# Layer 1's mixture of experts: where a block's outputs wait for their scatter

## The chip, the cores and the metric

The kernel runs on one core of a Trainium2 chip. The metric is the device time of one execution in microseconds, and lower is better. All data are float32. TensorE (PE) multiplies, VectorE (DVE) and ScalarE (ACT) do the elementwise work, GpSimd (POOL) mostly issues indirect DMAs here, and SyncE (SP) issues the direct ones.

## The reference

Four layers are computed in turn on 2708 rows of 256 numbers. Each layer first adds a graph product over the dense 2708 x 2708 adjacency matrix, and then a feed-forward part. The change lies in the feed-forward part of layer 1, a mixture of 8 experts with one hidden layer for all of them, in which every row goes through the expert with the greatest gate alone:

```python
def _L1_ffn_ref(x, W1, b1, Wg, bg, Wd, bd):
    H = jax.nn.gelu(xf @ W1 + b1, approximate=False)
    probs = jax.nn.softmax((H @ Wg + bg) / TEMP, axis=-1)
    assign = jnp.argmax(probs, axis=-1)
    out = jnp.zeros_like(xf)
    for e in range(Wd.shape[0]):
        y = H @ Wd[e] + bd[e]
        sel = (assign == e)[:, None]
        out = out + jnp.where(sel, probs[:, e:e + 1] * y, 0.0)
    return out.reshape(orig_shape)
```

`xf` is the layer-normalised `x`. It has 256 columns, `H` has 1024.

## The kernel before

**Layer 1.** The rows are worked in three groups (8, 8 and 6 tiles of 128 rows). For each group the graph product is summed in PSUM and added to `x`. Then `send1` normalises the rows (`normed`, which writes tiles `xn` of the pool `work`, three places in turn), turns them, computes `H` and the gate, writes the rows of `H` to a DRAM tensor `hid`, and decides where each row goes (`route`). For each row it scatters a pair, the row's number and its gate value, to the DRAM tensor `taken1` (L505), so that rows of one expert stand together.

**Blocks.** `blocks` cuts the experts' lists into blocks of 128 rows of one expert. Nine blocks (0 to 8) come from the first two groups, and their work begins while the third group is still in its gates. Fifteen more (9 to 23) come from the rest and need the third group's routing. A further set stands in a branch that is entered only if the number of blocks asks for it.

`Units.pieces` runs the blocks. For one block:

- `fetch_names` (L519, POOL) gathers the 128 pairs of row number and gate value;
- `fetch_rows` (L659, POOL) gathers the 128 rows of `hid` that they name into one of four buffers `hs`;
- `fetch` (L1054, SP) loads the expert's weights, 1152 KB with the bias in a last row, into one of three buffers `wb`. It first reads the expert's number;
- `turn` transposes the rows on PE (L670, eight transposes), and ACT copies them out of PSUM as `hTs` (L671). This is done one block ahead;
- 16 matmuls (L719) sum the 128 x 256 output in one of two PSUM banks `yacc`;
- DVE adds the bias from `wb` (L720) and multiplies by the gate value (L721). The result is `ys`, a tile of the pool of the blocks with two places in turn;
- POOL scatters its rows to the DRAM tensor `given1` (L505).

**What sets the order.** [...] A place in a pool is written again only when its last readers are done: `ys` when its scatter has landed, `hs` when the transposes of its rows are done, `wb` when L719 and L720 of its block are done. POOL issues names, rows and outputs from one queue, so an instruction that waits holds all behind it. Beside block 13 (`beside`, with n = NA + 4) PE and DVE do the few products of `centre` (L245) and DVE `score_columns` (L269, L270) for layer 2. Towards the end POOL also issues the loads of layer 2's small tensors. After the last block SP loads `given1` back (`mine`, L56), and the addition to `x` (L1413) begins layer 2. The tag `xn` is written in layer 1 by `norm_to` (L197) through `normed`; it is written again in layer 2.

Of the kernel before, what the change touches and what calls it, by code (L numbers as in the profile page):

```python
# [8 lines left out]
F32 = mybir.dt.float32  # L9
# [6 lines left out]
P = 128  # L16
N = 2708
D = 256
# [48 lines left out]
def adj_ffn4(ctx: ExitStack, tc: tile.TileContext, a: dict, out: bass.AP):  # L67
# [4 lines left out]
    work = ctx.enter_context(tc.tile_pool(name="work", reuse_waits="tile", bufs=3))  # L72
# [429 lines left out]
    def scatter(dst, ix, src, bound, group):  # L502


        i = g.indirect_dma_start(out=dst, out_offset=bass.IndirectOffsetOnAxis(ap=ix, axis=0),  # L505
                                 in_=src, in_offset=None, bounds_check=bound, oob_is_err=False)
        tc.declare_no_dep(i.ins, group=group, reason="different rows")
        tc.declare_no_dep(i.ins, group=group + "read", reason="rows that were read are not written")
        tc.add_to_no_dep_group(group, i.ins)
        scattered.setdefault(group, []).append(i.ins)  # L510
# [25 lines left out]
    class Blocks:  # L536
# [4 lines left out]
        def __init__(self, pool, given, weights):  # L541
            self.pool, self.given = pool, given
            self.weights, self.ahead, self.rows, self.at = weights, [], [], [0, 0]
            self.late, self.begun, self.made = None, None, None
            self.ik, self.ok = "taken0", "given0"
# [84 lines left out]
    class Units(Blocks):  # L630
# [3 lines left out]
        def __init__(self, pool, given, weights, hidden):  # L634
            Blocks.__init__(self, pool, given, weights)
            self.hidden, self.named, self.places, self.got = hidden, [], [0, 0], None

            self.names = pool.tile([P, MOST, 2], F32, name="names")
            g.memset(self.names, 1.0)
            self.hs = [pool.tile([P, HC * P], F32, name="hs", tag="hs", bufs=3) for _ in range(3)]  # L640
            for h in self.hs:
                g.memset(h, 0.0)
            self.ik, self.ok = "taken1", "given1"

        def fetch_names(self, item):
            (_, ix, *_), b, past, src, full = item
# [54 lines left out]
        def pieces(self, pool, during=None):  # L701

            turned = [self.turn(pool, self.rows[0][1])]
            yield
            n = 0
            while self.rows:
                if len(self.rows) > 1:
                    turned.append(self.turn(pool, self.rows[1][1]))
                    yield
                w2, hT = self.ahead.pop(0), turned.pop(0)  # L710
                m, _ = self.rows.pop(0)
                self.more()
                if during is not None:
                    during(n)
                n += 1
                y = pool.tile([P, D], F32, name="ys", bufs=2)
                q = pools["psum"].tile([P, W], F32, name="yacc", bufs=2)[:, :D]
                for f in range(HC):
                    te.matmul(q, lhsT=hT[:, f, :], rhs=w2[:, f, :], start=(f == 0), stop=(f == HC - 1))  # L719
                v.tensor_tensor(y, q, w2[:, HC, :], ALU.add)  # L720
                i = v.tensor_scalar(y, y, m[:, 1:2], None, op0=ALU.mult)  # L721
                self.last = i.ins.name
                scatter(self.given, m[:, 0:1].bitcast(I32), y, self.given.shape[0] - 1, self.ok)
                yield
# [60 lines left out]
    with ExitStack() as l0:  # L785
# [103 lines left out]
        for tiles in GROUPS:  # L889
# [8 lines left out]
            for j in range(FULL):  # L898
# [22 lines left out]
                y = gp.tile([P, GMAX * P], F32, name="y", bufs=3)[:r, :w]  # L921
# [440 lines left out]
    with tc.tile_pool(name="t3", reuse_waits="tile", bufs=1) as t3:  # L1362
# [279 lines left out]
        with tc.tile_pool(name="h2", reuse_waits="tile", bufs=2) as hp:  # L1642
# [120 lines left out]
            for c0, w in parts:  # L1763
# [11 lines left out]
                y = ypool.tile([P, 4, D], F32, name="y", bufs=2)  # L1775
# [11 lines left out]
        with tc.tile_pool(name="g3e", reuse_waits="tile", bufs=1) as ge, ExitStack() as sums:  # L1787
# [121 lines left out]
            for now, (m, j) in enumerate(slots):  # L1909
# [50 lines left out]
                for hf, (h0, q) in enumerate(halves):  # L1960
                    s.copy(oT[:, pair, hf, :q], num[:, hf, :q])
                    z, y = 2 * Q * hf, 2 * Q * pair
# [68 lines left out]
```

## The time and the profile before

| what | value |
|---|---|
| runs of the kernel before | 1935.83, 1922.75, 1929.87 us; median 1929.87 |
| profiled execution | 1912.16 us, its span 1910.4 us |
| PE, PE weight load | 1824.7 us (96%), 1323.7 us (69%) |
| DVE, ACT, POOL | 1098.8 us (58%), 642.4 us (34%), 343.8 us (18%) |
| first and last L719 | 953.6 and 1078.4 us after the span's start |
| first addition of layer 2 (L1413) | 1088.15 us |
| L720: count, median length | 24, 424 ns |
| L721: count, median length | 24, 353 ns |
| DMA from issue to landing, median: outputs, rows, names | 6.8, 7.7, 6.2 us (950 to 1086 us) |

Times of events are microseconds from the span's start. A line of the waits names the engine and the line that waited, what it waited for, the sum in us, the count and the longest. A wait for several semaphores is put down to the one that came last. In a line of the timeline the idle time before an instruction and its releaser stand in square brackets. [...]

### The profile page before, as it was taken

How to read it: one execution, taken by the hardware profiler on the slowest of the kernel's cores; microseconds unless marked ns; L12 is line 12 of the kernel's file. 1: busy time of each engine (PE TensorE's matmuls, PEld its weight loads, DVE VectorE, ACT ScalarE, POOL GpSimd, SP SyncE). 2: the span in 40 equal slices, each digit the busy share in tenths (PEclk: the TensorE clock that was granted, in tenths of full speed). 3: DMA queues.
4: the chain of work that ended last, by engine and by line, in shares of the span. 5: the costliest groups of instructions: out<-in, count | busy, mean ns of one | idle time of the engine just before them, and what ended most of it. 6: DMA issues, size and time to landing. Idle time of an engine off the chain costs nothing.

```text
span 1910.4 us, 25747 instructions
## 1 busy us (share of the span) xinstructions
PE 1824.7 (96%) x9453; PEld 1323.7 (69%) x9453; DVE 1098.8 (58%) x2498; ACT 642.4 (34%) x1459; POOL 343.8 (18%) x406
## 2 busy tenths in 40 slices
PE   7999999999998999999989799999899999999998
PEld 6888788888887888887778578887566632232344
DVE  6777873443333524454532365555354498999897
ACT  7868752222222303122312232222233551031231
POOL 1004254333321002304356200000000000000000
PEclk9999999999998999999999899999899999999999
DMA  8435657877763453644779610000101000000000
GB/s 273 142 110 156 217 191 287 333 299 294 287 255 127 151 151 101 162 116 121 215 259 360 216 40 1 1 1 1 44 1 34 17 1 23 23 15 26 20 20 16
DMA packets 90141, 243.94 MB, mean 128 GB/s; under 512 B 18159, under 2 KB 44823, under 8 KB 80792
## 3 DMA queue, kind: packets, MB, share of 16 engines
q1 hardware_dynamic: 73048, 199.80, 31.3%
q0 software_dynamic: 16960, 42.42, 6.8%
q8 instruction: 78, 1.28, 0.3%
q14 instruction: 55, 0.45, 0.1%
HBM read 216.29 MB, written 28.71 MB: 128 GB/s over the span
## 4 chain that ended last, share of the span: by engine, by line
PE 40%; DMA 4%; DVE 3%; ACT 2%; issue 1%; POOL 0%; DVEq 0%; POOLq 0%; SPq 0%; ACTq 0%
PE num L1929 10%; PE ps_acc L1502 9%; PE den L1939 6%; PE ps_tmp L367 4%; PE ps_acc L1692 3%; PE ps_tmp L260 2%; PE yacc L719 2%; DMA L_ffn_beta<-in_L_ffn_beta 1%; DMA given<-ys,names 1%; PE ps_acc L260 1%; PE ps_tmp L213 1%; DVE e L1899 1%; DMA names<-taken,b_ix 1%; DMA wb<-in_L_ffn_Wdp 0%; PE ps_acc L670 0%
## 5 line engine op out<-in xcount | busy, mean ns | idle before, releaser
L1899 DVE SCALAR_TENSOR_TENSOR e<-arena,G,mask 128x1024 f32<-128x1024 f32 (+1 forms) x264 | 286.9, 1147 | 13.7 <-PE den L1939 13.6
L1929 PE MATMUL num<-e,wh 128*64 128x512 f32 (+4 forms) x1056 | 215.8, 551 | 0.0
L929 PE MATMUL acc<-msg,wt 128*128 128x256 f32 x882 | 199.0, 382 | 2.8 <-DVE wt L887 1.5
L1502 PE MATMUL ps_acc<-hh,e 128*128 128x257 f32 x882 | 199.3, 382 | 1.9 <-ACT o L1445 1.9
L1290 PE MATMUL acc<-sup,adrow 128*128 128x256 f32 x882 | 198.4, 382 | 0.2 <-DVE adrow L1258 0.2
L929 PEld LDWEIGHTS acc<-msg,wt 128*128 128x128 f32 x882 | 165.5, 191 | 29.4 <-DVE wt L887 2.8
L1290 PEld LDWEIGHTS acc<-sup,adrow 128*128 128x128 f32 x882 | 164.8, 190 | 28.3 <-issue 5.5
L1502 PEld LDWEIGHTS ps_acc<-hh,e 128*128 128x128 f32 x882 | 163.7, 190 | 29.5 <-ACT o L1445 4.5
L583 PE MATMUL ps_acc<-xTs,wa 128*128 128x256 f32 (+1 forms) x768 | 169.4, 373 | 3.5 <-DVE xTs L573 3.4
L617 PE MATMUL yacc<-wb,hTs 128*128 128x256 f32 x736 | 168.4, 380 | 0.0
L585 ACT ACTIVATE hTs<-ps_acc,wa 128x256 f32<-128x256 f32 (+1 forms) x192 | 88.9, 465 | 236.1 <-PE yacc L617 161.9
L583 PEld LDWEIGHTS ps_acc<-xTs,wa 128*128 128x128 f32 x768 | 136.4, 190 | 29.9 <-DVE xTs L573 6.4
L1929 PEld LDWEIGHTS num<-e,wh 128*64 128x64 f32 (+1 forms) x1056 | 66.5, 136 | 127.3 <-issue 105.6
L617 PEld LDWEIGHTS yacc<-wb,hTs 128*128 128x128 f32 x736 | 137.1, 190 | 18.0 <-DVE ys L619 0.6
L1494 DVE SCALAR_TENSOR_TENSOR e<-Rb,G,mask 128x640 f32<-128x640 f32 (+2 forms) x110 | 85.0, 774 | 90.6 <-PE ps_acc L1502 90.4
L1939 PE MATMUL den<-e,wh 128*32 128x512 f32 (+4 forms) x1056 | 118.0, 548 | 0.0
L214 ACT COPY xT<-ps_tmp 128x256 f32<-128x256 f32 x98 | 33.6, 365 | 238.1 <-PE ps_tmp L213 218.9
L1255 DVE TENSOR_SCALAR mask<-adrow 128x1024 uint8<-128x1024 f32 (+1 forms) x66 | 41.1, 624 | 121.1 <-DMA adrow<-in_adjT 120.5
L719 PE MATMUL yacc<-wb,hTs 128*128 128x256 f32 x384 | 90.7, 391 | 12.3 <-DVE ys L720 7.8
L719 PEld LDWEIGHTS yacc<-wb,hTs 128*128 128x128 f32 x384 | 73.1, 195 | 24.1 <-DVE ys L720 8.8
L887 DVE SCALAR_TENSOR_TENSOR wt<-adrow,wt 128x640 f32<-128x640 f32 (+3 forms) x67 | 71.0, 1063 | 28.2 <-ACT wt L141 27.9
L1939 PEld LDWEIGHTS den<-e,wh 128*32 128x32 f32 (+1 forms) x1056 | 30.2, 108 | 77.9 <-issue 73.8
(457 smaller groups left out, 2562.6 us busy)
## 6 DMA issues: line engine op xcount, KB each, us to landing
adhalf<-in_adjT SPq DMA_DIRECT2D x42, 677.0 KB
wb<-in_L_ffn_W2p SPq DMA_DIRECT2D x24, 1152.0 KB
wb<-in_L_ffn_Wdp SPq DMA_DIRECT2D x24, 1152.0 KB
wa<-in_L_ffn_W1b SPq DMA_DIRECT2D x24, 1028.0 KB
adrow<-in_adjT SPq DMA_DIRECT2D x42, 512.0 KB
adrow<-in_adjT SPq DMA_DIRECT2D x42, 320.0 KB
adrow<-in_adjT SPq DMA_DIRECT2D x21, 576.0 KB
adrow<-in_adjT SPq DMA_DIRECT2D x21, 448.0 KB
```

The lines of the kernel that those rows point to most:

```text
L367: te.matmul(p[:, :w], lhsT=w1[:, c, f * P : (f + 1) * P], rhs=xnT[:, c, c0 : c0 + w], start=(c == 0), stop=(c == DC - 1))
L583: i = te.matmul(p[:, f % 2, : m * P], lhsT=w1[:, c, f * P : (f + 1) * P], rhs=xT[:, c, : m * P], start=(c == 0), stop=(c == DC - 1))
L585: s.activation(hT[:, f, : m * P], p[:, f % 2, : m * P], AF.Gelu, bias=bias[:, f : f + 1])
L617: te.matmul(q[:, k, :], lhsT=hT[:, f, k * P : (k + 1) * P], rhs=w2[:, f, :], start=(f == 0), stop=(f == HC - 1))
L719: te.matmul(q, lhsT=hT[:, f, :], rhs=w2[:, f, :], start=(f == 0), stop=(f == HC - 1))
L929: te.matmul(p[:q, n - pair[0], :], lhsT=wt[:, k : k + q], rhs=msg[:r, j, :], start=(j == 0 and n == pair[0]), stop=(j == FULL - 1 and n == ...
L1290: te.matmul(p[:q, n - pair[0], :], lhsT=ad[:, k : k + q], rhs=sup[:, jj, :], start=(jj == 0 and n == pair[0]), stop=(jj == FULL - 1 and n ...
L1494: i = v.scalar_tensor_tensor(e[:r, :w], Rb[:r, c0 : c0 + w], G[:r, j, :], mask[:r, j, c0 : c0 + w], op0=ALU.max, op1=ALU.mult)
L1502: te.matmul(p[:, : D + 1], lhsT=e[:, k : k + q], rhs=hh[:, j, :], start=(j == 0), stop=False)
L1899: v.scalar_tensor_tensor(e[:, :w], slow[:, m % 2, k, :w], G[:, j, 2 * pair + k, :], mask[:, j, c0 : c0 + w], op0=ALU.max, op1=ALU.mult)
L1929: te.matmul(num[k * DK : (k + 1) * DK, hf, :q], lhsT=wh[some, j, 2 * pair + k, :DK], rhs=e[some, h0 - c0 : h0 - c0 + q], start=(j == 0), s ...
L1939: te.matmul(den[z : z + Q, :q], lhsT=wh[some, i, 2 * pair + k, DK : DK + 1] .to_broadcast([some.stop - some.start, Q]), rhs=e[some, h0 - c ...
```

## The change

A counter of the blocks' outputs is kept. Of five outputs in turn, two are tiles `ys` of the pool of the blocks, as before, and three are tiles `xn` of the pool `work`, in whose three places the gates' normalised rows stood. Since `ys` has two places and `xn` three, an output's place is that of the output five blocks before it. No instruction is added or removed, and no transfer.

```diff
-            self.ik, self.ok = "taken1", "given1"
+            self.ik, self.ok, self.outputs = "taken1", "given1", 0
...
                 n += 1
-                y = pool.tile([P, D], F32, name="ys", bufs=2)
+                self.outputs += 1
+                y = (pool.tile([P, D], F32, name="ys", bufs=2) if self.outputs % 5 < 2 else
+                     work.tile([P, D], F32, name="xn"))
                 q = pools["psum"].tile([P, W], F32, name="yacc", bufs=2)[:, :D]
```

## The prediction

> **What bounds the kernel now.** I read the page for the span, the waits of the stretch from 950 to 1086 us (layer 1's blocks), then the timeline of TensorE in it, and last the windows of 5 us for the DMA engines' share. The page first:
>
> ```profile
> span 1910.4 us, 25747 instructions
> PE 1824.7 (96%) x9453; PEld 1323.7 (69%) x9453; DVE 1098.8 (58%) x2498; ACT 642.4 (34%) x1459; POOL 343.8 (18%) x406
> L719 PE MATMUL yacc<-wb,hTs 128*128 128x256 f32 x384 | 90.7, 391 | 12.3 <-DVE ys L720 7.8
> ```
>
> PE is the bound of the whole. The 384 matmuls of L719 are 24 blocks of 16, so the conditional rest did not run. A block costs PE 4.33 us in an undisturbed piece: 3.46 for L719 and 0.87 for the eight transposes of L670 (the chain of waits has both numbers). 24 of them are 103.9 us; the blocks take from 953.6 to 1078.8, 125.2 us. The waits say where part of the 21 us went (us in total, times, longest):
>
> ```profile
> DVE ys L720 <- DMA given<-ys,names: 63.3, 13, 8.8
> SPq L1054 <- DVE ys L720: 87.8, 18, 10.4
> PEld yacc L719 <- DVE ys L720: 8.8, 4, 5.3
> PE yacc L719 <- DVE ys L720: 7.8, 3, 5.0
> PE yacc L719 <- DMA wb<-in_L_ffn_Wdp: 4.5, 5, 1.7
> PE ps_acc L670 <- DMA hs<-hid,names: 2.2, 1, 2.2
> ```
>
> DVE's output of a block waits until the scatter of two blocks before has landed, for it has two places; the next weights (SPq L1054) wait for that output, because it reads the bias row of its weights; and PE, with two yacc banks, waits for it in turn. The timeline of PE (start, length, instructions, idle before and releaser) shows that only a few of the 13 waits reach PE:
>
> ```profile
> 987.45 1.04 PE L670 MATMUL ps_acc<-ident,hs 128*128 128x128 f32 x8
> 990.16 3.72 PE L719 MATMUL yacc<-wb,hTs 128*128 128x256 f32 x16 [1.67 <-DVE ys L720]
> 993.72 1.04 PE L670 MATMUL ps_acc<-ident,hs 128*128 128x128 f32 x8
> 999.80 6.58 PE L719 MATMUL yacc<-wb,hTs 128*128 128x256 f32 x16 [5.05 <-DVE ys L720]
> 1006.22 1.04 PE L670 MATMUL ps_acc<-ident,hs 128*128 128x128 f32 x8
> ...
> 1069.71 3.72 PE L719 MATMUL yacc<-wb,hTs 128*128 128x256 f32 x16 [1.04 <-DVE ys L720]
> 1075.10 3.69 PE L719 MATMUL yacc<-wb,hTs 128*128 128x256 f32 x16 [1.67 <-DMA wb<-in_L_ffn_Wdp]
> ```
>
> After the 5.05 us of idle time block 8's products take 6.58 us where others take 3.5. The windows (columns: busy time by engine, granted clock, DMA share, GB/s):
>
> ```profile
> 980.00:985.00 5.00, 4.96 (x25) 4.16 (x24) 0.78 (x2) 2.15 (x4) 2.87 (x3) 1.00 0.40 112
> 995.00:1000.00 5.00, 0.20 (x1) 0.20 (x2) 0.64 (x2) 0.48 (x1) 0.74 (x1) 0.88 0.45 170
> 1000.00:1005.00 5.00, 5.00 (x12) 4.00 (x13) 0.90 (x3) 0.00 (x0) 3.67 (x4) 0.50 0.83 298
> 1040.00:1045.00 5.00, 4.67 (x25) 4.03 (x26) 0.78 (x2) 1.35 (x4) 2.72 (x3) 1.00 0.99 405
> 1055.00:1060.00 5.00, 5.00 (x31) 4.45 (x29) 0.90 (x3) 1.53 (x3) 4.02 (x6) 1.00 1.02 420
> 1065.00:1070.00 5.00, 3.96 (x22) 3.33 (x22) 0.73 (x2) 1.64 (x4) 0.58 (x1) 1.00 0.70 289
> ```
>
> So there are three stages: up to 1005 DMA has gaps (0.40, 0.45) and PE waits for outputs; from 1005 to 1060 DMA is at 0.92 to 1.02; at the end it has gaps again.
>
> [...] clock 0.50 after 5.05 us, 1.00 after 1.67 us. [...]
>
> **The change, part by part.** Instructions of PE, ACT, SP and POOL stand in the same order before and after, with the same DMAs; on DVE, L720 and L721 only write elsewhere. No duration changes. What changes is one wait of L720: on the scatter of five blocks before instead of two.
>
> *First stage.* Block 6 ends on PE at 987.45. Then transposes 0.87, L719 of block 7 at 988.3 (before 990.16), end 991.8. The weights of block 7 were issued at 983.87, after L720 of block 4; that output's products ended at 979.8 (976.34 + 3.46, blocks counted from 0), so now at 980.3, 8.0 us ahead of use. Next late: the transposes of block 9. Their rows are gathered by POOL at 985.52, behind names that wait for the routing's scatters (landing 980.7); nothing of that moves. With the median 7.6 us of hs they land at 993.1 (4.5 to 10.5: 990.0 to 996.0). So transposes 993.1, block 8 at 994.0, end 997.4, against 1006.22: **-8.8 us**, of which 3.1 is the half clock. By the range of hs: -5.9 to -10 (PE alone would be there at 996.2).
>
> POOL hides behind that: an indirect DMA takes 1.02 + 0.31 us, three a block are 4.0, below PE's 4.33. It is behind at 984 (six routing scatters) and catches up. The new wait on five before: block 9's output (1001.9) needs the scatter of block 4, issued by POOL at 990.74, landed 999.2. It holds, with 2.7 us to spare; later ones have more.
>
> *Middle, blocks 9 to 20.* Before, 1007.10 to 1059.77 is 4.79 us a block at a DMA share of about 0.97. A block moves 1.18 MB weights, 0.52 rows, 0.13 outputs, 1.83 MB: at the 360 to 420 GB/s of full windows 4.4 to 5.1 us. So this stage is DMA's, not the output's; its waits of outputs (63.3 us, mostly here) are free. Two weight loads (blocks 9, 10) that were issued at 999.8 and 1000.6 go out at 987.9 and 992.3 now: 2.36 MB, 6.6 us of DMA at 360 GB/s. The gaps from 980 to 997.4 sum to 0.60x5 + 0.16x5 + 0.15x5 + 0.55x2.4 = 5.9 us. The 0.7 that doesn't fit, and rows that come late in the fuller queue, appear as waits for wb and hs: I take **+2 us**. Bounds: -2.8 (the four waits for wb there, 0.81 + 0.16 + 0.30 + 1.53, all gone) to +7 (both loads pushed through at full price).
>
> *End.* L720 of block 20 ran at 1069.23 though its products ended at 1063.4 (1059.77 + 3.6), behind the scatter of block 18 that POOL issued only at 1060.22, after five loads of layer 2. Now it runs at 1063.5, block 23's weights go out at 1064 instead of 1069.68 and land 5.4 us later, at 1069.4. Block 22 starts at 1068.5 (before 1069.71), block 23 at 1072, ends 1075.5 against 1078.8: **-3.3 us**; at least -1.2, at most -3.3. After that, the last scatter and the loads of layer 2 (1079.3 to 1088.2) are as before. xn is next written by ACT in layer 2's attention, long after the scatters landed: 0.
>
> Sum: -8.8 + 2 - 3.3 = **-10.1 us**, bounds -15.9 to -0.1. Against the profiled execution (1912.16, its span 1910.4) that is 1902. The median shown is 1929.87, 17.7 above that execution; nothing in the stages says the saving scales, so I subtract it: 1920.
>
> **Rivals.**
> *DMA is the bound throughout.* From 985 to 1075 its share sums to 80.2 of 90 us. If weights pushed into the first stage delay the hs of block 9 to 996 and the middle pays the full +7, the gain is 5.9 + 3.3 - 7, about 2: 1928. For it: the share of 1.0 after 1040. Against: gaps of 0.40 to 0.45 just where the loads move to. Chance 0.2.
> *PE alone is the bound.* If hs and wb are never late, the end lies at 953.6 + 103.9 + routing products 1.5, the L245 products 1.0, the wait for hs 2.6: 1062.6, a gain of 16: 1914. Against: full DMA windows need more than 4.33 us a block. Chance 0.1.
> *Slower: weights become late in every block.* A load may go out 9.0 us ahead of its use (two L719, three L670, less DVE's 0.5). In full windows it took 7.9 to 9.7 (issue 1032.13, use 1040.03; 1035.16, 1044.90). If the denser queue makes it 10.5, each of the 14 blocks from 9 to 22 waits 1.5: 21 us lost against 12.1 gained, 1939. It decides from 9.0 + 12.1/14 = 9.9 us. Against: the bytes are the same and waiting slows their issue. Chance 0.06.
> *It does nothing*, because the releaser was another (scatter and PE ends lie close): L720 started right after a landing 13 times, so hardly: 0.02, 1930.
>
> **How the numbers follow.** The forecast (gain 7 to 13) has 0.62. The likeliest time is 1920. The three times shown differ by 13 us, so I add about 4 either way to the cases: PE alone less 4 is 1910, DMA bound plus 2 is 1930: range 1909 to 1930. A difference under 1% (19 us) can't be told from none here. No case gains 19 without scatter of the runs: faster 0.08; slower 0.05; same 0.87.
>
> **What would show it.** Right: L720's waits for given near 0; no PE wait for ys; block 8 near 3.5 us at clock 1.0; waits for wb or hs up from 4.5 and 2.2; DMA share above 0.8 from 985 on; the first layer 2 addition near 1078 instead of 1088. Wrong: blocks 9 to 20 above 5.0 us each, or hs of block 9 landing after 996.

## The result and the profile after

| | before | after |
|---|---|---|
| median of 20 runs, us | 1927.05 (1918.82 to 1935.83) | 1921.84 (1916.06 to 1929.84) |
| ratio, 95% interval | | 0.997 (0.9957 to 0.9982) |
| profiled span, us | 1910.4 | 1916.0 |

The change is worth 5.8 us of 1927 by the ratio (3.5 to 8.3), a good half of the 10.1 forecast; the time lies 2 us from the 1920 predicted and well within the range. That closeness is luck in part: the forecast was taken off a median of 1929.87, 2.8 us above that of the 20 runs, and its gain was 4 to 5 us too large, so the two errors offset each other. The profiled execution of after is nevertheless 5.6 us longer than that of before. That contradiction is the first thing to clear up.

In after the lines from the products on have moved by two: L719 to L721 is L721 to L723, and L1054 is L1056. The page of after (first the span, then busy time by engine, then the row of the products):

```profile
span 1916.0 us, 25757 instructions
PE 1829.1 (95%) x9453; PEld 1327.3 (69%) x9453; DVE 1098.2 (57%) x2498; ACT 641.9 (34%) x1459; POOL 344.5 (18%) x406
L721 PE MATMUL yacc<-wb,hTs 128*128 128x256 f32 x384 | 88.9, 385 | 1.2 <-DMA wb<-in_L_ffn_Wdp 1.1
```

The idle time in front of the products fell from 12.3 us to 1.2, and none of it is an output's. The waits of after, 950 to 1086 us (total, times, longest):

```profile
DVE xn L722 <- PE yacc L721: 27.7, 8, 4.4
DVE ys L722 <- PE yacc L721: 23.5, 6, 7.0
PE ps_acc L670 <- ACT hTs L671: 7.4, 3, 3.8
PE yacc L721 <- DMA wb<-in_L_ffn_Wdp: 1.1, 1, 1.1
PE ps_acc L670 <- DMA hs<-hid,names: 0.9, 2, 0.7
```

L722 now mostly waits for its products. No line names a wait for `given`, where before had 63.3 us in 13 waits. But a line is there that before did not have: TensorE waits 7.4 us for `hTs`. The timeline of TensorE shows 5.8 us of it (columns as in the prediction):

```profile
982.31 1.04 PE L670 MATMUL ps_acc<-ident,hs 128*128 128x128 f32 x8
985.29 0.66 PE L670 MATMUL ps_acc<-ident,hs 128*128 128x128 f32 x4 [1.94 <-ACT hTs L671]
989.78 1.97 PE L670 MATMUL ps_acc<-ident,hs 128*128 128x128 f32 x8 [3.83 <-ACT hTs L671]
991.54 8.82 PE L721 MATMUL yacc<-wb,hTs 128*128 128x256 f32 x32
1000.20 0.60 PE L670 MATMUL ps_acc<-ident,hs 128*128 128x128 f32 x4
```

After 5.8 us of idle time (1.94 + 3.83) two blocks take 8.82 us, at a granted clock of 0.64 from 991.5 to 996.5, where the first profile of before has 7.07 at 1.00. I call this the stand. r5_before below, the kernel before unaltered, has it too. So it isn't the change's.

Nor is every output on time. Outputs 7, 8 and 10 begin 5.6, 2.0 and 1.6 us after the modelled end of their products:

```profile
DVE xn L722 <- PE ps_acc L670: 9.3, 2, 9.1
1014.20 0.42 DVE L722 TENSOR_TENSOR xn<-yacc,wb 128x256 f32<-128x256 f32 x1 [9.09 <-PE ps_acc L670]
```

This is output 7. A scatter hardly holds it: that of five blocks before was issued 27 us earlier. The trace has no update of TensorE's semaphore from 1004.7 to 1014.2, and then five within 0.35 us. That looks like a late signal of TensorE, and the stand does too.

**Profiles of two kinds.** All the profiles taken fall into two groups. In the first profile of before and in r9 to r12 (r9 to r12 on two chips) no such wait is seen, layer 0's blocks (first to last L583) take 334.8 to 336.2 us, and the trace holds 1455 or 1456 records of TensorE's semaphore. In after and in r1 to r8 (two chips for these eight runs) TensorE stands 4.5 to 5.9 us for `hTs` before block 4's products, layer 0's blocks take 345.7 to 349.1 us, and only 1423 to 1435 records are there. I call the groups N (no stand) and S (stand). The traces of S also lack 17 to 20% of the records of DMA landings (after has 9037, the first profile of before 11156), so what ended a wait is less sure there.

The 12 us of layer 0 look like a stand too. From 270 to 320 us TensorE is never idle in a profile of kind N. In each of the nine of kind S it is idle for 6.4 to 7.8 us and then works for 3.7 to 9.8 us at half clock; with half of these counted as lost, that is an estimate of 10 to 13 us. First a window of before, then two of r1_again:

```profile
295.00:300.00 5.00, 5.00 (x25) 4.27 (x24) 0.78 (x2) 1.90 (x4) 2.86 (x4) 1.00 0.67 197
295.00:300.00 5.00, 0.00 (x0) 0.00 (x0) 0.00 (x0) 0.00 (x0) 2.61 (x3) 0.76 0.62 242
300.00:305.00 5.00, 4.27 (x11) 3.51 (x12) 0.78 (x2) 0.00 (x0) 3.09 (x3) 0.55 0.27 76
```

The timed runs go with the chip: before took 1922 to 1927 us in the median where S was seen, 1907 to 1910 where N was. So the prediction read an execution of kind N, and its result was profiled in one of kind S; the two can't be subtracted. The table gives the stages that the prediction used, each from the trace: from the start of block 0's products to block 9's, on to block 21's, and to the end of the last.

| kernel | kind | 0 to 9 | 9 to 21 | 21 to end | sum |
|---|---|---|---|---|---|
| before, first profile | N | 53.49 | 57.08 | 14.62 | 125.18 |
| r12_before | N | 52.89 | 54.45 | 14.90 | 122.24 |
| r9_bias_before | N | 48.20 | 60.03 | 12.99 | 121.22 |
| r10_bias_after | N | 48.37 | 56.57 | 15.66 | 120.60 |
| r11_six | N | 49.80 | 59.79 | 12.38 | 121.98 |
| r5_before | S | 50.89 | 61.21 | 12.51 | 124.61 |
| r6_null | S | 51.02 | 57.69 | 14.69 | 123.41 |
| after | S | 51.19 | 55.53 | 12.71 | 119.43 |
| r1_again (after) | S | 49.61 | 58.64 | 12.89 | 121.14 |
| r2_early | S | 48.92 | 58.19 | 13.84 | 120.95 |
| r3_late | S | 50.49 | 56.42 | 12.80 | 119.70 |
| r4_three | S | 49.37 | 56.28 | 13.83 | 119.47 |

One kernel's stage differs by up to 3 us between two profiles of one kind (after and r1_again in the middle), so a stage of one profile is not read closer than that.

### The profile page after: what moved, and what is told of

Same layout as the page of the kernel before. It is cut to its first block, busy times and chain, and to the rows that moved or that the text cites. A ratio compares the mean times of both kernels' runs of the same rounds, so it can differ in the third digit from the quotient of the medians.

```text
span 1916.0 us, 25757 instructions
## 1 busy us (share of the span) xinstructions
PE 1829.1 (95%) x9453; PEld 1327.3 (69%) x9453; DVE 1098.2 (57%) x2498; ACT 641.9 (34%) x1459; POOL 344.5 (18%) x406
## 5 line engine op out<-in xcount | busy, mean ns | idle before, releaser
L1901 DVE SCALAR_TENSOR_TENSOR e<-arena,G,mask 128x1024 f32<-128x1024 f32 (+1 forms) x264 | 287.0, 1149 | 13.6 <-PE den L1941 13.6
L583 PE MATMUL ps_acc<-xTs,wa 128*128 128x256 f32 (+1 forms) x768 | 170.2, 374 | 5.4 <-DVE xTs L573 2.5
L583 PEld LDWEIGHTS ps_acc<-xTs,wa 128*128 128x128 f32 x768 | 137.1, 190 | 32.1 <-DVE xTs L573 5.4
L617 PEld LDWEIGHTS yacc<-wb,hTs 128*128 128x128 f32 x736 | 138.8, 193 | 24.4 <-issue 3.9
L721 PE MATMUL yacc<-wb,hTs 128*128 128x256 f32 x384 | 88.9, 385 | 1.2 <-DMA wb<-in_L_ffn_Wdp 1.1
L619 DVE TENSOR_TENSOR ys<-yacc,wb 128x256 f32<-128x256 f32 x46 | 19.5, 424 | 113.0 <-PE yacc L617 98.2
```

What stands on the lines that cost most here:

```text
L583: i = te.matmul(p[:, f % 2, : m * P], lhsT=w1[:, c, f * P : (f + 1) * P], rhs=xT[:, c, : m * P], start=(c == 0), stop=(c == DC - 1))
L617: te.matmul(q[:, k, :], lhsT=hT[:, f, k * P : (k + 1) * P], rhs=w2[:, f, :], start=(f == 0), stop=(f == HC - 1))
L1901: v.scalar_tensor_tensor(e[:, :w], slow[:, m % 2, k, :w], G[:, j, 2 * pair + k, :], mask[:, j, c0 : c0 + w], op0=ALU.max, op1=ALU.mult)
```

## The experiments

Blocks and outputs are numbered from 0, except that "the first nine outputs" are blocks 0 to 8. All ratios are to runs of the kernel before on the same chip.

### Which outputs bring the gain: r1 to r4

r1_again is the change unaltered. The others change only the choice of the place:

```diff
# r2_early: five places for the first nine outputs only
-  ... if self.outputs % 5 < 2 else
+  ... if self.outputs % 5 < 2 or self.outputs > 9 else
# r3_late: five places from the tenth output on
+  ... if self.outputs % 5 < 2 or self.outputs <= 9 else
# r4_three: three places, all of them xn
+  y = work.tile([P, D], F32, name="xn")
```

> The changed kernel once more, unaltered, for a second profile of the first stage: in the first one PE stood from 983 to 991.5 us between the outputs of blocks 3 and 4 and nothing in that view says for what. If that stall belongs to the change (weights pushed into a full DMA queue), it is there again, of 4 to 8 us, and the blocks take about 119 us from the first L721 to the end of the last. If it is an accident of one execution, it is gone and the blocks take 111 to 115 us. Time in either case 3 to 8 us below the kernel before.

> Five places for the first nine outputs only, two for the rest. Theory (first stage gains most): 2 to 5 us below the kernel before, block 8 without idle time for an output before it. Rival (DMA is the bound throughout, and what the first stage gains is paid back in the middle): 0 to 1 us below the kernel before. Rival (the end gains it): 0.

> Two places for the first nine outputs, five from the tenth on. Theory: only the end gains, 1 to 3.3 us below the kernel before, and the wait of 5 us with the half clock before block 8 is as in the kernel before. Rival (DMA throughout): nearly the whole gain of the change, 4 to 6 us, is here.

> Three places for all outputs, those of the normalised rows alone. Theory: a third place already takes away most of it, since a scatter lands 6.8 us (4.0 to 8.5) after its issue and a block takes 4.3 to 4.8; but where POOL is behind by up to 10 us, around block 6, part of the wait stays: 2 to 5 us below the kernel before, between it and the five places. If five places are needed all along, it is within 1 us of the kernel before.

| run | ratio | 95% interval |
|---|---|---|
| r1_again | 0.9980 | 0.9969 to 0.9992 |
| r2_early | 1.0017 | 1.0005 to 1.0029 |
| r3_late | 0.9972 | 0.9959 to 0.9984 |
| r4_three | 0.9979 | 0.9968 to 0.9989 |

On this chip, one of kind S, no gain is seen from the places of the first nine outputs, on which the prediction's largest term rested: r2 is 3.3 us slower (1.0 to 5.6), which isn't read as a loss, since r6 below leaves up to 4 us between two builds of one program. The later ones are worth all of it, 5.4 us. Both results go against the theory in their expectations, and r3 has the gain that the rival there named. A third place is already as good as five within the intervals. r3_late, which keeps two places up to block 8, has the stand too:

```profile
PE ps_acc L670 <- ACT hTs L671: 5.8, 1, 5.8
PE yacc L721 <- DMA wb<-in_L_ffn_Wdp: 3.7, 4, 1.2
```

In r3 outputs 6 and 8 still come 4.9 and 4.1 us after their products, but TensorE waits only 0.17 us for an output (before block 8; in the first profile of before output 6 came 11.7 us late, and the wait was 5.05). That POOL and the scatters catch up while TensorE stands is the likely reason; it wasn't tested.

### Is the stand the change's, and what can two builds differ by: r5 and r6

r5_before is the kernel before, unaltered. r6_null gives its two places as two tags of one place each; instructions and waits are those of before:

```diff
-  y = pool.tile([P, D], F32, name="ys", bufs=2)
+  y = pool.tile([P, D], F32, name="ys", tag=f"ys{n % 2}", bufs=1)
```

> The kernel before once more, for a second profile. All four profiles taken since show PE standing 5.8 us before the second half of block 6's transposes, which the first profile of the kernel before does not have, and so does the one whose first nine outputs use the places of before. If that stall is the kernel's own and the first profile of before was a lucky draw, it is here too, and the blocks take 124 to 132 us here from the first L719 to the end of the last. If the stall comes from the change, it is absent.

> The kernel before with its two places under two names, the same instructions and waits at other addresses, to see what a build alone is worth. If builds of the same program agree, 0 within 0.1 per cent of the kernel before. If the layout alone moves the time by 3 us either way, the differences among the runs so far can't be read to better than that.

r5_before took 1926.75 us (one run) beside 1925.82. r6_null measured 0.9995 (0.9979 to 1.0011). So a difference below some 3 us between builds can't be told from none with this number of runs, and the 5.8 us of the change are not much above it. The waits of TensorE and SP in r5_before:

```profile
PE yacc L719 <- DMA wb<-in_L_ffn_Wdp: 5.9, 5, 3.3
PE ps_acc L670 <- ACT hTs L671: 4.5, 1, 4.5
PE yacc L719 <- DVE ys L720: 0.7, 1, 0.7
SPq L1054 <- DVE ys L720: 82.6, 18, 9.2
```

The stand is there without the change. Outputs hold TensorE for 0.7 us only, against 7.8 in the first profile, but weights hold it for 5.9 (r6_null: 6.5). After has 1.1 of this, r1_again 1.2, r2_early, with two places for the later blocks, 4.3. In kind S, then, these profiles have an output's late scatter reach TensorE over SP: L720 waits for the scatter, the next load waits for L720 because a place of `wb` holds the bias too, and TensorE waits for the load.

### Is the full DMA queue the condition: r7 and r8

Half of the expert's weights, so that a load moves 640 KB instead of 1152:

```diff
-  wb = wbs["pool"].tile([P, 2048 + D], F32, name="wb", bufs=3)
+  wb = wbs["pool"].tile([P, 1024 + D], F32, name="wb", bufs=3)
-  te.matmul(q, lhsT=hT[:, f, :], rhs=w2[:, f, :], ...)
+  te.matmul(q, lhsT=hT[:, f, :], rhs=w2[:, f % 4, :], ...)
-  v.tensor_tensor(y, q, w2[:, HC, :], ALU.add)
+  v.tensor_tensor(y, q, w2[:, 4, :], ALU.add)
```

The lines are shown in part; the load is shortened to match. These two kernels leave out half of the weights, and the bias too, in whose stead a piece of the weights is added.

> The kernel before with half of each block's weights left out (four of the eight 128-row pieces are loaded and used twice), so that a block moves 1.3 MB instead of 1.83. Theory (waits for outputs cost PE beside DMA's bound): the waits of L720 for scatters stay, a scatter lands in 3 to 5 us, and the blocks take 110 to 120 us. Rival (DMA is the bound throughout): the blocks drop to PE's 104 to 110 us with two places already.

> The changed kernel with the same half of the weights left out. Theory: with DMA relieved the places are worth more than the 4 to 5 us of the whole kernels, 6 to 12 us below the halved kernel before. Rival (DMA throughout, so that the queue of transfers makes the scatters slow in the first place): less than with the whole weights, 0 to 3 us, since scatters land soon enough for two places.

r7 (two places) measured 0.9957 (0.9939 to 0.9975), r8 (five) 0.9961 (0.9945 to 0.9978): with half the bytes no gain from the places is seen, though the intervals leave room for up to 4 us. r8's theory, 6 to 12 us, is refuted; its rival's 0 to 3 fits. The blocks took 114.0 us in r7's profile, within its theory's 110 to 120, but the waits for scatters, which that theory kept, are nearly gone. A window of r7 and its wait for the scatters:

```profile
1010.00:1060.00 50.00, 48.94 (x270) 43.25 (x269) 12.07 (x33) 13.66 (x24) 34.28 (x34) 1.00 0.80 267
DVE ys L720 <- DMA given<-ys,names: 5.4, 1, 5.4
```

At a DMA share of 0.80, where r5_before has 0.94 in the same window, one output is seen to wait for a scatter, not 11 (49.4 us in r5_before). That supports the reading that two places were too few because scatters land late while the weights load. A profile of kind N agrees: in r12 the last two scatters, with no weights left to load (DMA share 0.11 and less), landed in 2.4 and 2.6 us, those of blocks 3 to 17, where the trace has them, in 5.4 to 6.9 (DMA share 0.99 from 1010 to 1060). Taking 12 MB away (24 times 512 KB) gave 8 us only by the ratio, so the bytes don't bound the whole stretch.

### Is it the weights' release: r9 to r11

r9 has two places, but the bias has a tile and a load of its own (four places), so that `wb` is freed by TensorE alone. r10 is the same edit on the changed kernel. r11 has six places, three `ys` and three `xn`. The lines are shown in part:

```diff
-  wb = wbs["pool"].tile([P, 2048 + D], F32, name="wb", bufs=3)
+  wb = wbs["pool"].tile([P, 2048], F32, name="wb", bufs=3)
+  bd = wbs["pool"].tile([P, D], F32, name="bd", bufs=4)
+  i = nc.sync.dma_start(bd, a["L1_ffn_Wdp"][bass.ds(e, 1), :, 2048:] ...)
-  v.tensor_tensor(y, q, w2[:, HC, :], ALU.add)
+  v.tensor_tensor(y, q, bd, ALU.add)
# r11_six
+  y = (pool.tile([P, D], F32, name="ys", bufs=3) if self.outputs % 6 < 3 else
```

> The kernel before, two output places, but the bias row of an expert has a tile and a load of its own (four places, 128 KB, the same bytes in all), so that a place of the weights comes free when TensorE has read it (L719) and no longer when L720 has. L720 still waits for the scatter of two blocks before. Theory A (the five places gain through the earlier release of the weights): TensorE's waits for wb fall from 4.5 to 5.9 us to below 2, and the time is 3 to 6 us below the kernel before (ratio 0.997 to 0.998). Theory B (they gain through L720 releasing the yacc banks, or through the order on DVE): no gain, within 2 us of the kernel before; waits for wb may fall, but waits of TensorE for yacc (ys) or hs take their place. Theory C (one more transfer a block on a full queue costs by itself): 2 to 6 us above.

> The changed kernel (five places) with the same separate bias tile. Theory A: nothing is left to gain, since L720 already runs right after its products: within 2 us of the changed kernel, ratio to the kernel before 0.996 to 0.999. Theory B: likewise about the changed kernel. Theory C: 2 to 6 us above the changed kernel, ratio 0.999 to 1.001. Against r9, Theory A has the two equal within 2 us, Theory B has this one 4 to 6 us lower.

> Six places in turn, three of them ys and three of them xn; nothing else is changed against five. If with five places no output waits for a scatter any more (none did in the profile of the changed kernel), this is the changed kernel again: ratio 0.996 to 0.998. If five still hold an output back in executions other than the profiled one, another 2 us or more comes off: below 0.996.

| run | places | ratio | 95% interval |
|---|---|---|---|
| r9_bias_before | 2 | 0.9983 | 0.9972 to 0.9993 |
| r10_bias_after | 5 | 0.9969 | 0.9956 to 0.9981 |
| r11_six | 6 | 0.9975 | 0.9965 to 0.9986 |

The weights' release alone gives 3.2 us of the 5.9 that r10 gives. Six places give 4.8 us, no more than five gave elsewhere (0.9970 and 0.9980), as its expectation has it. No version here is shown to beat the change. In r9 TensorE's waits for `wb` are down to 0.5 us, as Theory A has it, and the ratio lies just outside the ones it named. It still waits 4.5 us for outputs (before: 7.8, r12: 5.8) and 3.2 for rows. The middle values make the release half of the gain; the intervals leave anything from a sixth to all of it. r9's profile shows what stays when only the weights are freed. SP waits for TensorE now; then DVE's timeline, with two outputs that wait for scatters, the second ahead of layer 2's `score_columns`; and last TensorE:

```profile
SPq L1054 <- PE yacc L719: 70.0, 20, 9.8
```

```profile
1009.22 0.42 DVE L720 TENSOR_TENSOR ys<-yacc,bd 128x256 f32<-128x256 f32 x1 [4.98 <-DMA given<-ys,names]
...
1018.63 0.42 DVE L720 TENSOR_TENSOR ys<-yacc,bd 128x256 f32<-128x256 f32 x1 [3.52 <-DMA given<-ys,names]
1019.09 0.35 DVE L721 TENSOR_SCALAR ys<-ys,names 128x256 f32<-128x256 f32 x1
1019.36 0.75 DVE L269 TENSOR_TENSOR o<-w_l,L_gnn_attn_src 128x256 f32<-128x256 f32 x2
```

```profile
1021.82 2.09 PE L245 MATMUL ps_tmp<-w_l,all_ones 128*128 128x258 f32 x4 [4.18 <-DVE w_l L270]
```

L269 stands behind an L720 that waited 3.52 us for a scatter and began at 1018.63; it begins at 1019.36, and TensorE waits 4.18 us for the scores. So a late output has three ways to TensorE, the `yacc` bank, the weights, and whatever follows L720 on DVE; in r10, with five places, TensorE waits by none of them.

r10 and r11 are also the first profiles of kind N with more than two places, that is, of the execution that the prediction had worked out. TensorE in r10, from block 7 to block 9, and the windows of 5 us beside it:

```profile
989.16 3.62 PE L721 MATMUL yacc<-wb,hTs 128*128 128x256 f32 x16
997.46 1.94 PE L670 MATMUL ps_acc<-ident,hs 128*128 128x128 f32 x8 [4.68 <-DMA hs<-hid,names]
999.19 4.43 PE L721 MATMUL yacc<-wb,hTs 128*128 128x256 f32 x16
1003.46 1.04 PE L670 MATMUL ps_acc<-ident,hs 128*128 128x128 f32 x8
1004.34 3.62 PE L721 MATMUL yacc<-wb,hTs 128*128 128x256 f32 x16
```

```profile
982.40:987.40 5.00, 5.00 (x27) 4.41 (x26) 0.78 (x2) 1.07 (x2) 3.07 (x3) 1.00 1.00 355
987.40:992.40 5.00, 5.00 (x28) 4.44 (x28) 0.78 (x2) 1.07 (x2) 2.39 (x3) 1.00 0.96 358
992.40:997.40 5.00, 0.38 (x2) 0.00 (x0) 0.79 (x2) 0.00 (x0) 2.63 (x3) 1.00 0.98 324
997.40:1002.40 5.00, 4.94 (x20) 4.46 (x21) 0.00 (x0) 1.17 (x2) 2.09 (x3) 0.66 0.62 235
```

The wait for the output before block 7 or 8 is gone, as predicted. In its place TensorE waits 4.68 us for the rows of block 9, almost as long as the 5.05 us for the output before, and its clock falls as it did (0.66 in the last window; 4.43 us for a block). The windows are 26.4 us after block 0's start, like those from 980 on in before: the DMA shares, 0.40, 0.84, 0.85 and 0.45 there, have become 1.00, 0.96, 0.98 and 0.62.

### Was the 5 us wait of the first profile an accident: r12

The kernel before, unaltered, for one more profile.

> The kernel before, unaltered, for one more profile: the first profile of before and r5_before differ in the first stage, and the profiles of r9, r10 and r11 (all 1452 semaphore records of TensorE, no wait of 4 to 6 us for hTs) resemble the first one. If this execution is of the kind of r9 to r11, Theory 1 (with two places the third scatter of that stretch is late and TensorE stands 5 us for it) expects block 9 to begin 52 to 54 us after block 0 as in the first profile (53.5), against 48.4 in r10 and 49.8 in r11; Theory 2 (the 5.05 us of the first profile were that execution's own) expects 48 to 50. If it is of the kind of r5_before, it shows a wait of 4 to 6 us for hTs instead and says nothing on this.

It ran on a chip of kind N (1910.21 us, beside 1906.79) and block 9 began 52.9 us after block 0, as Theory 1 has it. TensorE in it:

```profile
999.61 6.26 PE L719 MATMUL yacc<-wb,hTs 128*128 128x256 f32 x16 [4.39 <-DVE ys L720]
```

So with two places the wait for the output before block 8 belongs to kind N (5.05 and 4.39 us). It isn't in r5_before, where the stand came first.

## Why the prediction was right, and where it was not

The time fell within the range and on the forecast's side. No rival came about as a whole. But of the three terms the first is half its size at best, and the other two measured no more than the scatter between profiles.

**The first stage, -8.8 us: the term that was mis-sized.** In kind N, block 9 starts 53.2 us after block 0 with two places (mean of two profiles) and 49.1 with five or six (r10, r11): -4.1. That isn't the places' doing alone: r9, with two places and the weights freed earlier, has 48.2, and its waits for outputs before blocks 7 and 8 are 1.67 and 1.76 us. In kind S it is 51.0 (r5, r6) against 50.4 (after, r1): -0.6.

The step that failed in kind N is "nothing of that moves", said of the names and rows of block 9. The prediction found the next late thing rightly, and the two loads did go out early: 32.5 and 36.8 us after block 0 in r10, where it had 34.3 and 38.7 and before had 46.2 and 47.1. But POOL's small transfers landed later beside them. The names of block 9 landed 2.4 us after their issue in both profiles of before of kind N, at a DMA share of 0.40 and 0.31 in these 5 us, and 4.6, 5.1 and 5.8 in r9, r10 and r11, where the share was 1.00 (r10) and 0.94 (r11); so the gather of the rows went out at 33.4 us after block 0 (r10) and 33.8 (r11) instead of 31.9, and took 8.1 and 8.7 us instead of the 7.6 assumed. It landed at 41.5 and 42.5, not 39.5. That costs 2.0 and 3.0 us.

The long wait brought back the half clock that the sum had saved (granted clock 0.66 and 0.50 in the windows after it): transposes of 1.94 us for 1.04 and products of 4.43 and 4.85 for 3.62, 1.7 and 2.1 us. Together 3.7 and 5.1: block 8 ends 47.5 and 48.9 us after block 0 (at the next transposes) where the forecast had 43.8. That is outside the term's own range, 5.9 to 10 us: its late end, rows at 996.0, left 4.2 us of idle time and yet no half clock. The sum had no term for names that land late, in 5.1 and 5.8 us against 2.4 in these profiles. What the rival of a bound DMA said of this stage, rows at 996 (42.4 us after block 0), was nearly exact; its +7 us in the middle was not paid. In kind S, where the result was timed, the names of block 9 took 6.4 to 7.5 us (six profiles) with two places and with five, and the stand replaced the wait that this term was to remove.

**The middle, +2 us.** In kind N the stretch from block 9 to 21 went from 55.8 to 58.2, +2.4, with waits for `hs` in the place of those for `wb`, as predicted: after block 9 r10 has 2.8 us of them, r11 5.1, and neither waits for `wb`. In kind S it went from 59.5 to 57.1, -2.4: there the waits for weights fell from about 6 us to about 1. Both sizes are within the 3 us by which single profiles differ. "Its waits of outputs are free" sits badly with r3, which gained 5.4 us (3.1 to 7.9) in kind S by the outputs from block 9 on alone.

**The end, -3.3 us.** -0.7 in kind N (14.8 to 14.0) and -0.8 in kind S (13.6 to 12.8). Single profiles run from 12.4 to 15.7, so no more is said than that the full 3.3 is not seen. In r10 the last block waits 2.34 us on SP's side and then takes 5.38 us for 3.62 (granted clock 0.90 from 1060 to 1080).

The sums of these means are -2.4 us (N) and -3.7 (S) of the blocks' stretch. The timed gain was 3.8 to 5.9 us (r1, after, r11, r10). In kind S the trace accounts for most of it; in kind N it is short by about half, no more than the scatter between profiles.

**Rivals.** That TensorE alone bounds the stretch is refuted by the 119 us and more that it takes in every version with all the weights, against 109. Slower by late weights: waits for weights fell. That the change does nothing: the waits for `given` are gone. That DMA is the bound throughout: right on the rows of block 9 in kind N; its +7 us in the middle isn't seen, and with half of the weights' bytes the time fell by 8 us only.

**Readings and sums.** The 13 waits for scatters (63.3 us) stood on DVE; TensorE waited for outputs three times (7.8 us). By its own terms the lower bound of the sum is -16.1, not -15.9.

**The gap that should have been read.** The sum was made against an execution 17.7 us below the median of the runs, and the text let that stand. Of it, about 12 us are layer 0's blocks, which stand in the other kind, and the first stage is different too. The single profile was true of some chips, and not of the one that gave the times.

**Left open.** What makes the stand. In it ACT and DVE resume within 0.2 us of each other; DVE's output 3 begins 6.3 to 6.7 us after its products ended by the trace. In all nine profiles of kind S that is 4.2 to 4.5 us after POOL's part in the last routing scatter ended, and in layer 0's stand DVE resumes 3.3 to 3.6 us after it. That points to these scatters, but kind N has them without a stand, and output 7 of after is late with none of them near. They weren't taken away in any run. Whether recording the trace has a part in it isn't known either: the traces that have the stand are those that lack records. The release of the weights (r9) was tried on a chip of kind N only, so the path over SP in kind S is read from profiles. Nor was "only the early places" run on a chip of kind N, so how much of the gain there is the first stage's is read from profiles alone.

## What to carry to other kernels

When a place is added, work out not only which wait ends but which transfers start earlier, and count what they delay, above all the small transfers that the next step needs: here a wait of 5 us for an output became one of 4.7 for rows. Look for every resource that the waiting instruction holds (a bank, a buffer with two readers, the engine's own order), since the smallest one may be the one that reaches the bound engine. And when a profiled execution lies 1% from the median of the runs, take a second profile of the kernel before any single wait is priced.

## What the runs showed of the hardware

The same kernel has two kinds of execution, by the chip as far as four chips tell: 1907 to 1910 us or 1922 to 1927 (medians, or single runs), about 12 us of which lie in layer 0's blocks (334.8 to 336.2 against 345.7 to 349.1), at nearly the same mean granted clock (0.98 to 0.99). In the longer kind TensorE stands once in each of two layers, 4.5 to 5.9 us for `hTs` in layer 1 and 6.4 to 7.8 us in layer 0, and in after DVE begins output 7 5.6 us after the modelled end of its products. A late signal of TensorE would fit the stand of layer 1 and output 7; it was not shown. The trace of that kind lacks some 20 to 30 records of TensorE's semaphore and a fifth of those of DMA landings.

A gather of 1 KB, the names of block 9, took 2.4 us to land in kind N at a DMA share of 0.40 (before) and 0.31 (r12), and 5.1 and 5.8 at 1.00 (r10) and 0.94 (r11). POOL's indirect DMAs kept the order of its queue: in the first profile of before a gather of rows waited 19.18 us for transposes, and the three behind it followed 1.30 to 1.35 us apart.

TensorE's granted clock fell after long idle times. In before it was 0.50 from 1000 to 1005 after 5.05 us (products of 6.58 us), in r12 0.52 in the same window after 4.39 (6.26), in r10 0.66 from 997.4 to 1002.4 after 4.68 (4.43), in after 0.64 from 991.5 to 996.5 after 1.94 and 3.83 (8.82 for two blocks). After 1.67 us it stayed at 1.00 in before (990 to 995; products of 3.72). In between the length alone doesn't decide: after 2.05 us (r1) and 2.08 (r11) transposes took 1.76 and 1.80 us for 1.04 and products 4.64 and 4.60 for 3.62, but after 2.22 (before) two blocks took 7.07, as at full clock, and after 3.13 (r8) the last four matmuls of a block took 1.03, the next transposes 1.04. What decides there was not shown.
